# The last wo chunk's parts and the next rows' last quarter in VectorE's order, in a two-layer graph kernel

## The chip, the cores and the metric

The kernel runs on one core of a Trainium2 chip. The metric is the device time of one execution in microseconds. Before the change it is 2554.0 us, the median of three runs (2552.22 to 2556.43); the profiled execution has a span of 2553.1 us at a granted TensorE clock of 0.995.

## The reference

64 graphs of 256 nodes with 512 features, one adjacency matrix, two layers, each with a residual and a LayerNorm. Layer 0 is masked attention with 8 heads, layer 1 a plain graph convolution:

```python
q = (x @ Wq + bq).reshape(b, n, H, HD)          # k and v alike
scores = jnp.einsum('bqhd,bkhd->bhqk', q, k) / jnp.sqrt(jnp.float32(HD))
scores = scores + (1.0 - adj)[None, None, :, :] * -1000000000.0
attn = jax.nn.softmax(scores, axis=-1)
out = jnp.einsum('bhqk,bkhd->bqhd', attn, v).reshape(b, n, d)
x = layernorm(x + out @ Wo + bo)
y = jnp.einsum('nm,bmd->bnd', adj, x)
x = layernorm(x + jnp.einsum('bnd,do->bno', y, weight) + bias)
```

Everything is float32.

## The kernel before, in words

**Precision.** The five weight products (v, q, k, wo and the last weight l) are made of parts. An operand is cut into a high part, a low part (the remainder, scaled) and a correction called diff, all in the round float format that TensorE takes. A product of 512 columns is then three products that add up in one PSUM bank: low times one weight part, high times another, diff times the third. `near` (L317) issues the first two, twelve or eight matmuls in groups of four, and has ScalarE scale the bank (L326); `far` (L328) issues the third and evicts the bank. For wo and l the eviction is VectorE's: `r += bank` with a sum for the LayerNorm (L338); at the fourth chunk `norm` follows, whose first step is the mean (L436) and whose squares run on ScalarE (L444).

**Parts.** For wo and l the stationary operand is the attention's output or the convolution's, cut in four chunks. `chunk_parts` (L284) makes a chunk's parts with three VectorE operations, cut (L168), clow (L169) and cdiff (L174), and ScalarE's copy of the cut is chigh (L298). The pools hold one `cut`, three chunks of chigh and clow, and four cdiff. For v, q and k the operand is the transposed input of the pair: `x_t` transposes a quarter (L264), `x_parts` cuts it (L168, L169), `x_diff` (L174) makes its third part; ScalarE copies its high part (L278).

**Work and its order.** Two graphs make a pair, and there are 32 pairs. A window w (of 1 to 30) works on three pairs at once: wo and the convolution of pair w - 1, attention of pair w, and v, q, k of pair w + 1, with the parts of pair w + 2's input. Attention is four units (two groups of heads by two graphs). For a unit, `scores` (L359) puts eight matmuls in each of two halves (L367), ScalarE takes the exponentials (L371), and VectorE multiplies each half by the adjacency mask (L376, `masked`), then adds the halves (L382, `summed`). `values`, at the next unit's slot, sums that over the keys on TensorE (L394), multiplies with v (L402) and divides on VectorE (L412 to L418).

**Who decides the order.** In the windows 1 to 30 the order on TensorE, ScalarE and VectorE is that in which the program issues (a manual schedule). `between(w)` (L540) writes the steps of a window as one list. `block` is one near plus whatever `far` has been owed for longest (up to two stay owed); `caught_up(1)`, the step f1, pays all but one. After a block, a slot or a convolution step comes a tick; `later(n, f)` runs f at the nth tick. That places the masks: the first half's mask at the tick right after the slot, the second's one tick later (L372), the sum one tick after that. `PENDING` carries the fourth quarter of the next input's parts from one window into the next (three steps; twelve in window 1).

**Around the change.** A window begins with the slot of unit 0, then the parts of wo's third chunk (`co[2:3]`), the block of chunk 0, f1 (which pays the third product of the last l chunk of the previous pair, called l3 here), the parts of wo's last chunk (`co[3:]`), the block of chunk 1, the pending quarter, and the blocks of chunks 2 and 3. Four PSUM banks serve all these products in turn, four others serve scores and values.

Of the kernel before, what the change touches and what calls it, by code (L numbers as in the profile page):

```python
# [43 lines left out]
def fast(tc, x, adj, wq, bq, wk, bk, wv, bv, wo, bo, w1, b1, out):  # L44
# [6 lines left out]
    NP = B // 2  # L51
# [78 lines left out]
    def raw_weight(name, tiles, queue):  # L130

        for i in range(3):
            SCRATCH[name, i] = scratch.tile([P, DC, D], F32, name=f"{name}{i}")
        n = DC // len(tiles)
        for i, t in enumerate(tiles):
            for k in range(n):
                RAW[name, i * n + k] = t[:, k]
            w = SOURCE[name][i * n * P:(i + 1) * n * P]
            if name == "o":


                for a in range(n):
                    queue.dma_start(t[:, a], w.rearrange("(h a i) e -> a h i e", h=4, a=2)[a])
            else:
                queue.dma_start(t, w.rearrange("(c p) e -> p c e", p=P))
# [79 lines left out]
    def later(n, f, *args):  # L225
        due.append([n, f, args])
# [132 lines left out]
    def scores(p, u):  # L359
        g, b = UNITS[u]  # L360
        for kc in range(NC):

            sc = [ps_at.tile([P, 2, N], F32, name="at") for s in range(2)]
            for a in range(2):
                for s in range(2):
                    r = slice(s * HD, (s + 1) * HD)
                    nc.tensor.matmul(sc[s][:, a, :], K[p, g][r, a, b, kc * P:(kc + 1) * P], Q[p, g][r, a, b, :],  # L367
                                     start=True, stop=True)
            e = E[p, u, kc] = one.tile([P, 2, 2, N], F32, name=f"e{kc}")
            for s in range(2):  # L370
                nc.scalar.activation(e[:, s], sc[s], AF.Exp, scale=qscale)  # L371
            later(1 + kc, masked, p, u, kc)  # L372

    def masked(p, u, kc):
        e = E[p, u, kc].rearrange("p s a n -> p (s a) n")
# [164 lines left out]
    def between(w):  # L540

        ahead, behind = w + 1, w - 1
        b = lambda name: [(block, name, behind if name in "ol" else ahead, j) for j in range(4)]
        v, q, k, o, l = (b(n) for n in "vqkol")
        c = lambda name, p: [(chunk_parts, name, p, j) for j in range(4)]
        y = [(adj_x, behind, i) for i in range(4)]
        bo_steps = [(with_bo, w, b) for b in range(2)]
        x_steps = [(x_t, w + 2, i) for i in range(4) if w + 2 < NP]
        x1 = [[s for f in (x_t, x_parts) for s in [(f, w + 2, i)] if w + 2 < NP] for i in range(4)]
        x2 = [[(x_diff, w + 2, i)] if w + 2 < NP else [] for i in range(4)]  # L550
        slot, f1 = [None], [(caught_up, 1)]
        f0 = [(caught_up,)]
        split = lambda name: [(split_w, name, i) for i in range(4)]
        mixed = lambda m, n: [s for pair in zip(m, n) for s in pair]
        halves_tiles = lambda: [one.tile([P, 2, D], F32, name=f"hl{i}") for i in range(2)]
        if w == -1:
            return [(x_t, 0, i) for i in range(4)] + mixed(v, split("v")) + mixed(q, split("q")) + [(adj_t,)] + \
                mixed(k, x_steps)
        if w == 0:
            raw_weight("o", halves_tiles(), nc.sync)  # L560
            PENDING[:] = [s for m, n in zip(x1, x2) for s in m + n]
            return slot + mixed(v, split("k")) + slot + q[:3] + split("o") + [(bv_wo,), (load_w, 3)] + \
                [(lambda: raw_weight("l", halves_tiles(), nc.sync),)] + slot + q[3:] + k[:2] + split("l") + \
                [(load_r, 0)] + slot + k[2:] + bo_steps + c("o", w)[:2] + \
                [(load_w, 3), (load_r, 1)]
        co, cl = c("o", behind), c("l", behind)
        seq = slot + co[2:3] + o[:1] + f1 + co[3:] + o[1:2] + PENDING[:6] + o[2:] + PENDING[6:] + slot + v + q[:1] + slot + q[1:] + f1 + \
            y[:1] + f0 + y[1:2] + k[:1] + (cl[:1] if w < NP - 2 else []) + y[2:] + f0 + bo_steps + slot + k[1:2] + \
            (cl[1:2] if w < NP - 2 else [])
        PENDING[:] = x1[3] + x2[3]  # L570
        if w == NP - 2:
            co = c("o", w)
            return seq + k[2:3] + co[:1] + k[3:] + co[1:2] + [(block, "o", w, 0)] + cl[:1] + [(block, "o", w, 1)] + cl[1:2]
        seq += k[2:3] + cl[2:3] + k[3:] + x1[0] + l[:1] + f1 + x2[0] + x1[1] + x2[1] + l[1:2] + cl[3:] + \
            l[2:3] + c("o", w)[:1] + x1[2] + x2[2] + l[3:] + f1 + c("o", w)[1:2]
        return seq

    PENDING = []

    def slot(before, unit):  # L580
        if before[0] >= 0:
            values(*before)
        scores(*unit)
# [11 lines left out]
    def window(w):  # L595
        steps(between(w), [(w - 1, 3)] + [(w, u) for u in range(4)])
# [235 lines left out]
```

## Time and profile before

| | |
|---|---|
| time, median of three | 2554.0 us |
| span of the profiled execution | 2553.1 us |
| busy: TensorE, VectorE, ScalarE, GpSimd | 2496.0, 1872.6, 1705.7, 382.4 us |
| moved | 600.25 MB, mean 235 GB/s |
| TensorE's wait for clow, whole run | 24.6 us in 33 times, longest 2.2 us |
| mean of a mask (L376), of a residual (L338) | 1221, 687 ns |
| mean of a 128x512 wo or l matmul | 391 to 401 ns |

Busy time counts what an engine executed; a matmul's row is longer than the distance to the next one, since matmuls are pipelined. A row of a timeline gives start, length, engine, line and operation, output and inputs with their shapes, the number of instructions merged, and in brackets the idle time before it and what ended it. A row of the waits gives who waited for whom, the time in total, how often, and the longest.

### The profile page before, as it was taken

To read this page: it belongs to the slowest core of one execution; us is meant where nothing else is said; L and a number is where in the kernel's file an instruction comes from. 1 tells how busy PE (TensorE), PEld (TensorE's weight loads), DVE (VectorE), ACT (ScalarE), POOL (GpSimd) and SP (SyncE) were. 2 spreads that over 40 slices of the span, in tenths; PEclk is the share of its full clock that TensorE was granted. 3 is DMA by queue.
4 is the path that set the end of the run, shared out by engine and by line. 5 is a ranking of instruction groups with operands and counts; after the bars stand their busy time and mean duration, and the time that the engine had idled before them with its cause. 6 is when DMAs were issued, how large, how long until landed. Compare 5 with 4: busy or idle time off the path is not lost.

```text
span 2553.1 us, 42184 instructions
## 1 busy us (share of the span) xinstructions
PE 2496.0 (98%) x15806; PEld 1886.6 (74%) x15806; DVE 1872.6 (73%) x3239; ACT 1705.7 (67%) x3206; POOL 382.4 (15%) x793
## 2 busy tenths in 40 slices
PE   8999999999999999999999999999999999999997
PEld 4477777777777777777777777777777777777765
DVE  4676787677886677876767876768876778866786
ACT  4557666776666766666776667766667766677755
POOL 0111111111111111111111111111111111111101
PEclk9999999999999999999999999999999999999998
DMA  7868778778788687777787787787787787777711
GB/s 205 284 201 273 235 232 259 240 244 243 240 256 247 236 263 232 235 250 252 231 274 226 232 259 243 240 262 234 246 246 247 251 247 233 247 254 229 257 68 51
DMA packets 375744, 600.25 MB, mean 235 GB/s; under 512 B 273520, under 2 KB 273776, under 8 KB 317552
## 3 DMA queue, kind: packets, MB, share of 16 engines
q0 software_dynamic: 65232, 475.03, 51.9%
q1 hardware_dynamic: 309760, 121.42, 22.0%
q8 instruction: 127, 2.08, 0.3%
q10 hardware_dynamic: 544, 1.05, 0.1%
q14 instruction: 81, 0.66, 0.1%
HBM read 548.15 MB, written 49.28 MB: 234 GB/s over the span
## 4 chain that ended last, share of the span: by engine, by line
PE 70%; DVE 25%; issue 3%; DMA 1%; ACT 0%; POOL 0%; SPq 0%; DVEq 0%; ACTq 0%
PE mm L314 50%; PE at L367 7%; PE at L402 6%; PE mm L512 5%; DVE clow L169 4%; DVE r L338 3%; DVE cdiff L174 3%; DVE diff L174 2%; DVE cut L168 2%; PE at L394 2%; DVE e L376 2%; DVE low L169 2%; DVE xT L264 2%; DVE x L168 1%; DVE o L418 1%
## 5 line engine op out<-in xcount | busy, mean ns | idle before, releaser
L326 ACT ACTIVATE mm<-mm 128x512 f32<-128x512 f32 x616 | 357.8, 581 | 356.7 <-PE mm L314 356.6
L376 DVE TENSOR_TENSOR e<-e,adjT 128x1024 f32<-128x1024 f32 x256 | 307.6, 1221 | 34.2 <-ACT e L371 34.2
L314 PE MATMUL mm<-wr,clow 128*128 128x512 f32 x1024 | 285.1, 401 | 25.1 <-DVE clow L169 24.6
L371 ACT ACTIVATE e<-at 128x512 f32<-128x512 f32 x512 | 265.2, 604 | 52.9 <-PE at L367 52.9
L314 PE MATMUL mm<-wr,chigh 128*128 128x512 f32 x1024 | 279.9, 396 | 0.7
L314 PE MATMUL mm<-wr,cdiff 128*128 128x512 f32 x1024 | 269.6, 391 | 5.9 <-ACT mm L326 5.9
L314 PE MATMUL mm<-low,wr 128*128 128x512 f32 x960 | 265.1, 398 | 0.0
L314 PE MATMUL mm<-high,wr 128*128 128x512 f32 x960 | 257.2, 390 | 0.0
L367 PE MATMUL at<-qT,kT 64*128 64x256 f32 x2048 | 256.6, 389 | 0.1
L314 PEld LDWEIGHTS mm<-wr,clow 128*128 128x128 f32 x1024 | 188.7, 190 | 86.6 <-DVE clow L169 38.3
L314 PE MATMUL mm<-diff,wr 128*128 128x512 f32 x960 | 248.5, 391 | 0.0
L402 PE MATMUL at<-e,v 128*32 128x256 f32 x4096 | 246.9, 381 | 0.0
L367 PEld LDWEIGHTS at<-qT,kT 64*128 64x128 f32 x2048 | 190.6, 186 | 67.7 <-issue 53.0
L499 DVE TENSOR_TENSOR hl<-r,hl 128x512 fp32r<-128x512 f32 x122 | 84.3, 691 | 203.4 <-ACT hl L498 203.4
L314 PEld LDWEIGHTS mm<-wr,chigh 128*128 128x128 f32 x1024 | 191.5, 189 | 53.0 <-ACT chigh L298 14.2
L314 PEld LDWEIGHTS mm<-wr,cdiff 128*128 128x128 f32 x1024 | 192.5, 188 | 48.1 <-ACT mm L326 7.8
L444 ACT ACTIVATE z<-r,mean 128x512 bf16<-128x512 f32 x240 | 172.6, 719 | 76.2 <-DVE mean L436 71.2
L314 PEld LDWEIGHTS mm<-low,wr 128*128 128x128 f32 x960 | 173.6, 188 | 51.6 <-issue 19.9
L338 DVE SCALAR_TENSOR_TENSOR r<-mm,r 128x512 f32<-128x512 f32 x240 | 160.4, 687 | 69.6 <-PE mm L314 69.6
L314 PEld LDWEIGHTS mm<-high,wr 128*128 128x128 f32 x960 | 180.3, 188 | 38.4
L476 ACT ACTIVATE r<-r,less,rstd 128x512 f32<-128x512 f32 x248 | 200.4, 808 | 6.1 <-DVE less L469 6.1
L314 PEld LDWEIGHTS mm<-diff,wr 128*128 128x128 f32 x960 | 176.3, 188 | 33.6
(123 smaller groups left out, 3985.0 us busy)
## 6 DMA issues: line engine op xcount, KB each, us to landing
wr<-o POOLq DMA_DIRECT2D x93, 1024.0 KB, 6.3
wr<-v POOLq DMA_DIRECT2D x90, 1024.0 KB, 6.4
wr<-q POOLq DMA_DIRECT2D x90, 1024.0 KB, 6.5
wr<-k POOLq DMA_DIRECT2D x90, 1024.0 KB, 7.3
wr<-l POOLq DMA_DIRECT2D x90, 1024.0 KB, 7.6
x<-in_x_dram SPq DMA_DIRECT2D x496, 64.0 KB, 6.4
r<-in_x_dram SPq DMA_DIRECT2D x31, 1024.0 KB, 5.3
out_dram<-r SPq DMA_DIRECT2D x60, 512.0 KB, 6.5
```

Source lines behind the costliest of these rows:

```text
L169: nc.vector.tensor_tensor(low, a, cut, op=OP.subtract)
L174: nc.vector.scalar_tensor_tensor(diff, low.bitcast(F32), -(FINE + 1), a, op0=OP.mult, op1=OP.add)
L314: nc.tensor.matmul(pm, *operands(name, p, j, i, k), start=k == 0 and i == begins, stop=k == DC - 1, skip_group_check=True)
L326: nc.scalar.activation(pm, pm, AF.Copy, scale=1 + 1 / FINE)
L338: nc.vector.scalar_tensor_tensor(r, pm, 1.0, r, op0=OP.mult, op1=OP.add, accum_out=ST[p, name][:, j:j + 1])
L367: nc.tensor.matmul(sc[s][:, a, :], K[p, g][r, a, b, kc * P:(kc + 1) * P], Q[p, g][r, a, b, :], start=True, stop=True)
L371: nc.scalar.activation(e[:, s], sc[s], AF.Exp, scale=qscale)
L376: nc.vector.tensor_tensor(e, e, mask[:, kc:kc + 1, :].to_broadcast([P, 4, N]), op=OP.mult)
L402: nc.tensor.matmul(at[h * 32:(h + 1) * 32, a, :], V[p, b][:, kc, col:col + 32], e[kc][:, h % 2, h // 2, :], start=kc == 0, stop=kc == NC - 1)
L444: nc.scalar.activation(waste, R[p][j // 2][:, j % 2], AF.Square, bias=mean[:, j:j + 1], accum_out=squares[:, j:j + 1])
L476: nc.scalar.activation(r, r, AF.Identity, scale=rstd, bias=less)
L512: nc.tensor.matmul(pm[:, j, :], hl[:, i, mc, j * P:(j + 1) * P], adjT[:, mc, :], start=mc == 0 and i == 0, stop=mc == NC - 1 and i == 1)
```

## The change

Two edits. In windows whose pair is 2 to 30, the second mask of the first unit comes at the third tick instead of the second, so it falls behind the second block; and the parts of the last wo chunk are issued ahead of f1, so directly behind the third chunk's on VectorE. With the mask, the sum goes one tick later too. The pending quarter of the next rows' parts goes behind the block of chunk 2 instead of behind that of chunk 1; window 1, where twelve steps are pending, keeps its places. The purpose is to have the last chunk's parts ready when TensorE comes to its block.

```diff
@@ scores
-            later(1 + kc, masked, p, u, kc)
+
+            later(1 + kc * (1 + (u == 0 and 1 < p < NP - 1)), masked, p, u, kc)
@@ between
+        x_now = (PENDING[:6], [], PENDING[6:]) if w == 1 else ([], PENDING[:], [])
         co, cl = c("o", behind), c("l", behind)
-        seq = slot + co[2:3] + o[:1] + f1 + co[3:] + o[1:2] + PENDING[:6] + o[2:] + PENDING[6:] + slot + v + q[:1] + slot + q[1:] + f1 + \
+        seq = slot + co[2:3] + o[:1] + co[3:] + f1 + o[1:2] + x_now[0] + o[2:3] + x_now[1] + o[3:] + x_now[2] + slot + v + q[:1] + slot + q[1:] + f1 + \
             y[:1] + f0 + y[1:2] + k[:1] + (cl[:1] if w < NP - 2 else []) + y[2:] + f0 + bo_steps + slot + k[1:2] + \
             (cl[1:2] if w < NP - 2 else [])
```

## The prediction

> **What bounds the kernel now.** I read the page's busy times first, then who waited for whom on TensorE, then the chain of waits in order of time, then the timelines of TensorE, VectorE and ScalarE through one window. A window is one pair of graphs; its start repeats every 77.37 us (TensorE's stall of 1066.42 returns at 1143.80), and the middle 29 windows (w = 2 to 30) are alike.
>
> ```profile
> PE 2496.0 (98%) x15806; PEld 1886.6 (74%) x15806; DVE 1872.6 (73%) x3239; ACT 1705.7 (67%) x3206; POOL 382.4 (15%) x793
> ...
> PE 70%; DVE 25%; issue 3%; DMA 1%; ACT 0%; POOL 0%; SPq 0%; DVEq 0%; ACTq 0%
> ```
>
> TensorE is nearly always busy, yet a quarter of the chain lies on VectorE: somewhere in each window TensorE hands the chain to VectorE and takes it back. TensorE's waits between 500 and 2000 us, some 19.4 windows, name the place; this is the whole answer:
>
> ```profile
> PE mm L314 <- DVE clow L169: 12.1, 20, 0.6
> ```
>
> One wait per window, 0.6 us, and nothing else. The timeline of TensorE shows what is held:
>
> ```profile
> 1062.93 1.07 PE L314 MATMUL mm<-wr,clow 128*128 128x512 f32 x4
> 1063.84 1.07 PE L314 MATMUL mm<-wr,chigh 128*128 128x512 f32 x4
> 1064.74 1.07 PE L314 MATMUL mm<-wr,cdiff 128*128 128x512 f32 x4
> 1066.42 1.20 PE L314 MATMUL mm<-wr,clow 128*128 128x512 f32 x4 [0.61 <-DVE clow L169]
> 1067.65 1.19 PE L314 MATMUL mm<-wr,chigh 128*128 128x512 f32 x4
> 1068.68 1.08 PE L314 MATMUL mm<-wr,cdiff 128*128 128x512 f32 x4
> 1069.69 0.64 PE L394 MATMUL at<-sm,ones 128*32 128x256 f32 x8
> ```
>
> The first three rows are chunk 2 of wo (near, then the third product of chunk 0), the next three chunk 3 (near, then the third product of chunk 1), the last the next unit's sums of exponentials. Groups in flow start 0.91 us apart. The stall costs more than 0.61: chunk 3 should start at 1064.74 + 0.91 = 1065.65 and starts 0.77 later; its chigh group starts 1.23 after clow (ScalarE writes chigh only at 1066.98 to 1067.60), 0.32 too late; the refill adds 0.12 to cdiff. Without any wait L394 would come at 1065.65 + 0.91 + 0.91 + 1.0 = 1068.46 (the last step as in the row, 1068.68 to 1069.69). So the window loses 1.23 us. VectorE over the same stretch:
>
> ```profile
> 1062.67 0.69 DVE L174 SCALAR_TENSOR_TENSOR cdiff<-clow,o 128x512 fp32r<-128x512 f32 x1
> 1063.28 1.22 DVE L376 TENSOR_TENSOR e<-e,adjT 128x1024 f32<-128x1024 f32 x1
> 1064.42 0.68 DVE L338 SCALAR_TENSOR_TENSOR r<-mm,r 128x512 f32<-128x512 f32 x1
> 1065.03 0.08 DVE L338 DVE_READ_ACCUMULATOR r<-mm,r 128x1 f32 x1
> 1065.14 0.17 DVE L436 TENSOR_SCALAR mean<-sums 128x4 f32<-128x4 f32 x1
> 1065.22 0.42 DVE L168 TENSOR_SCALAR cut<-o 128x512 int32<-128x512 int32 x1
> 1065.67 0.69 DVE L169 TENSOR_TENSOR clow<-o,cut 128x512 fp32r<-128x512 f32 x1
> 1066.40 0.69 DVE L174 SCALAR_TENSOR_TENSOR cdiff<-clow,o 128x512 fp32r<-128x512 f32 x1
> 1067.01 1.22 DVE L382 TENSOR_TENSOR sm<-e,e 128x1024 f32<-128x1024 f32 x1
> ```
>
> VectorE has no gap here: chunk 3's low part stands behind the second mask (L376), the previous pair's last residual (L338, "r of l3" below) and the mean. Its stretch began when TensorE released a buffer to it at 1045.31 (the wait "DVE diff L174 <- PE mm L314", 28 times, 0.33 us each). So the two engines keep their distance from window to window, and what TensorE gains at L394 is gained in the period, if nothing between L394 and the next 1045.31 + 77.37 is tighter.
>
> **What the skill says.** The Trainium skill, "PSUM — Partial Sum Buffer", section "Engine vs sequencer instructions": VectorE's and ScalarE's queues are strict FIFO and matmuls start and complete in program order. The trace agrees: cdiff of chunk 1, ready since the last window, sits behind clow of chunk 3 till 1068.68. "Perfetto Trace Analysis", section "DVE / Act Engine Instruction": an instruction's end is its write acknowledged, and the semaphore's way to the others lies outside. Here clow starts at 1065.67, ends at 1066.36 and TensorE starts at 1066.42: 0.06 us more. "VectorE: DVE Perf Modes", section "The DRAIN you can't avoid", says that the next operation waits for the pipe to empty; the trace shows starts 0.61 us apart for a 128x512 operation followed by an independent one and 0.73 before its consumer, although each row says 0.69. I count starts.
>
> **The change, part by part.** It removes and adds no instruction. TensorE, GpSimd and the DMA queues keep their order. In windows 2 to 30 (u = 0 and 1 < p < 31) VectorE's order becomes: parts of chunk 2, parts of chunk 3, r of l3, mean, second mask, r of chunk 0, sum, then the next rows' last quarter (xT, x, low, diff), r of chunk 1. On ScalarE chigh of chunk 3 comes before the first two squares instead of behind them, and the copy of the next rows' high part behind the scaling of chunk 3 instead of in front of it. Window 1 keeps its order, since its mask is not delayed and its pending steps stay put.
>
> VectorE from 1063.28, with the starts measured above (cut 0.45, clow 0.73, cdiff 0.61, r 0.61, read accumulator 0.11, mean 0.08, mask 1.14): cut 1063.28, clow 1063.73, cdiff 1064.46, r of l3 1065.07, mean 1065.79, mask 1065.87, r of chunk 0 1067.01, and, behind its accumulator read, which took nothing extra between two residuals earlier in the trace, the sum at 1067.62. Do the moved ones wait? Cut needs chigh of chunk 2 read (ScalarE 1061.94 to 1062.58, past). Clow takes the buffer of chunk 0 (three of them), free by about 1060.3. Cdiff takes that of l3 (four), read by TensorE at 1060.21 to 1061.28. r of chunk 0 needs cdiff of chunk 0, done at 1065.81. None waits.
>
> Chunk 3 is then ready: clow at 1064.42; chigh on ScalarE directly behind the scaling at 1063.13, so at about 1063.7 to 1064.3. The 0.77 and the 0.32 fall away. Two other waits appear.
>
> First, chunk 3 takes the PSUM bank of l3 (four banks in turn: l3, chunks 0, 1, 2), which r of l3 frees. Before, that was done at 1065.1; now it starts at 1065.07 and releases TensorE 0.75 later (as clow did, 1065.67 to 1066.42), at 1065.82: 0.17 behind 1065.65. With one refill (1.03) L394 would come at 1065.82 + 1.03 + 0.91 + 1.0 = 1068.76.
>
> Second, L394 needs the sum. Before it had ended at 1068.23, 1.46 early; now it starts at 1067.62, 0.61 later, because r of chunk 0 was put in front of it. In the one place where the trace shows TensorE waiting for a sum, it started at 115.01 and L394 at 116.37: 1.36. So L394 comes at 1067.62 + 1.36 = 1068.98, the later of the two. Behind L394 stand the values, the scores of unit 1 and the whole rest, all in TensorE's queue. The gain is 1069.69 - 1068.98 = 0.71 us per window, times 29 = 20.6 us. Bounds: if the sum releases 0.2 sooner, the bank's 1068.76 holds (0.93, 27 us); if each of the seven moved operations costs 0.04 more, as dependent pairs do, 0.43 (12.5 us).
>
> The later block for the next rows' quarter costs nothing: its low part now starts at 1069.96 instead of 1069.35, and v reads it after the scores, at about 1073.2. ScalarE: the mean is 0.65 later, so the four squares and both scalings run from 1066.06 to 1070.22, the high part to 1070.74, zc to 1071.1; vc is wanted at 1071.4 (L402's end, 0.71 earlier than 1072.1). That margin shrinks from 1.1 to 0.3 us but stays. VectorE's lag behind TensorE is taken up by its waits of 0.27 and 1.49 us at 1074 to 1077. Weights and rows are as before: TensorE waits for no transfer in these windows.
>
> **Rivals.** *Full gain:* if VectorE's sum and r of l3 release sooner than I count, the whole 1.23 us goes: 35.7 us, 2518. For it: 0.5 us decides. Against: the queue has no gap to draw in. *The wait only changes hands:* the sum, or vc on ScalarE with its thin 0.3 us, comes later still and L394 or the scores hold most of what chunk 3 gave: 0 to 0.4 us per window, 2542 to 2554. For it: VectorE is continuously busy from 1045 to 1074, and the same work stands before L394, with one residual more. *Slower:* the moved parts wait in front of the mask. If clow of chunk 3 had to wait for chunk 2's buffer (TensorE done with it at 1064.8), all behind it comes 1.07 later, the sum releases L394 at 1070.05, 0.36 later than before: 29 x 0.36 = 10 us, 2564. Against: the buffers are counted above.
>
> **How the numbers follow.** My forecast, 0.4 to 1.0 us per window, 0.62: 2554.0 - 20.6 = 2533.4. Full gain 0.15, hands changed 0.15, slower 0.08. 0.2% is 5.1 us, 0.18 us per window; half of the third case passes it: faster 0.85, same 0.09, slower 0.06. The range 2518 to 2548 leaves out part of the full gain, the weak half of the third case and the slower one, about 0.2.
>
> **What would show it.** Right: the wait for clow gone from TensorE in windows 2 to 30; in its place about 0.2 us at L394 for the sum (L382), perhaps a trace of a wait for r (L338); a period of 76.66 us; VectorE's and TensorE's busy times unchanged. Wrong: no wait at L394 (then full gain), waits of scores on ScalarE's vc, VectorE idle before a cut or clow, or TensorE waiting for clow of chunk 2, which has only 0.25 us to spare (ready at 1062.63, read at 1062.93).

## The result and the profile after

The changed kernel takes 2539.22 us (median of four, 2537.62 to 2540.18) against 2555.22 us for the kernel before in the same comparison: ratio 0.9938, 95% interval 0.9921 to 0.9956, 16.0 us faster. The forecast was 2533.4 us, 20.6 us faster; the direction and the place were right, the gain was taken 4.6 us too large.

The page of the changed kernel, busy times and chain by engine:

```profile
PE 2492.1 (98%) x15806; PEld 1896.3 (75%) x15806; DVE 1870.2 (74%) x3239; ACT 1708.7 (67%) x3206; POOL 382.5 (15%) x793
...
PE 70%; DVE 25%; issue 3%; ACT 1%; DMA 0%; POOL 0%; DVEq 0%; SPq 0%; ACTq 0%
```

Busy times are as before, and so are the chain's shares: TensorE still hands the chain to VectorE in each window. What it waits for there has changed. TensorE's waits from 500 to 2000 us, the whole answer:

```profile
PE at L395 <- DVE sm L383: 0.5, 3, 0.2
PE mm L314 <- DVE r L338: 0.2, 1, 0.2
```

The 12.1 us for clow are gone; a sum and a residual are named instead, but only where the gap in the matmul rows is wide enough to be counted. The weight loads name the residual in every window; from the same stretch:

```profile
PEld mm L314 <- DVE r L338: 11.3, 20, 0.6
```

The regular form shows in TensorE's timeline (lines after L371 have moved by one):

```profile
1059.35 1.07 PE L314 MATMUL mm<-wr,cdiff 128*128 128x512 f32 x4
1060.56 1.20 PE L314 MATMUL mm<-wr,clow 128*128 128x512 f32 x4
1061.60 1.08 PE L314 MATMUL mm<-wr,chigh 128*128 128x512 f32 x4
1062.52 1.08 PE L314 MATMUL mm<-wr,cdiff 128*128 128x512 f32 x4
1063.72 0.64 PE L395 MATMUL at<-sm,ones 128*32 128x256 f32 x8
```

Two short stalls stand where one long one was. Chunk 3's clow group comes 1.21 us behind the group ahead, where flow is 0.91: 0.30 for the bank of l3. L395 comes 1.20 behind the last group, where flow is 1.0: 0.20 for the sum. VectorE's rows over the same stretch:

```profile
1057.27 0.69 DVE L174 SCALAR_TENSOR_TENSOR cdiff<-clow,o 128x512 fp32r<-128x512 f32 x1
1057.88 0.42 DVE L168 TENSOR_SCALAR cut<-o 128x512 int32<-128x512 int32 x1
1058.40 0.69 DVE L169 TENSOR_TENSOR clow<-o,cut 128x512 fp32r<-128x512 f32 x1
1059.20 0.69 DVE L174 SCALAR_TENSOR_TENSOR cdiff<-clow,o 128x512 fp32r<-128x512 f32 x1
1059.81 0.68 DVE L338 SCALAR_TENSOR_TENSOR r<-mm,r 128x512 f32<-128x512 f32 x1
...
1060.62 1.22 DVE L377 TENSOR_TENSOR e<-e,adjT 128x1024 f32<-128x1024 f32 x1
1061.75 0.68 DVE L338 SCALAR_TENSOR_TENSOR r<-mm,r 128x512 f32<-128x512 f32 x1
...
1062.36 1.22 DVE L383 TENSOR_TENSOR sm<-e,e 128x1024 f32<-128x1024 f32 x1
```

Cdiff of the third chunk starts at 1057.27 here and at 1062.67 in the profile before; I use this offset of 5.40 us to put both on the clock of before. The order is the forecast one and there is no gap. But clow starts 0.52 after cut, not 0.45, and cdiff 0.80 after clow, not 0.73. Everything behind is 0.14 to 0.15 late: r of l3 at 1065.21 (worked out: 1065.07), the sum at 1067.76 (1067.62), L395 at 1069.12 (1068.98).

The period, taken from one window's bias row (`r<-r,bo`) to the next, falls from 77.37 to 76.80 us: 0.57 times 29 windows is 16.5 us. The profiled spans differ by 15.8, since the first such row comes 0.9 us later in this profile (120.12 against 119.23), a start that lies between 117.9 and 121.4 in all the profiles here.

The question left is the 0.14 us. Theory A: clow and cdiff of the last chunk must each see that TensorE has done with an old buffer. Both buffers are long free, but the wait is one more entry in VectorE's queue. The chain of waits of the changed kernel, from the third chunk's cdiff on, has rows of that kind, DVEq (start, length, what; those around them are left out):

```profile
1058.34 0.02 DVEq L169
...
1058.40 0.70 DVE clow L169
...
1059.14 0.02 DVEq L174
...
1059.20 0.69 DVE cdiff L174
```

Theory B: the loss comes from the bank of l3, TensorE's 0.30, taken as 0.31 below. A second question is whether bank and sum are all that is left.

### The profile page after: what moved, and what is told of

Read it like the earlier page. It is cut to its first block, busy times and chain, and to the rows that moved or that the text cites. A ratio compares the mean times of both kernels' runs of the same rounds, so it can differ in the third digit from the quotient of the medians.

```text
span 2537.3 us, 42184 instructions
## 1 busy us (share of the span) xinstructions
PE 2492.1 (98%) x15806; PEld 1896.3 (75%) x15806; DVE 1870.2 (74%) x3239; ACT 1708.7 (67%) x3206; POOL 382.5 (15%) x793
## 4 chain that ended last, share of the span: by engine, by line
PE 70%; DVE 25%; issue 3%; ACT 1%; DMA 0%; POOL 0%; DVEq 0%; SPq 0%; ACTq 0%
PE mm L314 49%; PE at L367 7%; PE at L403 6%; PE mm L513 5%; DVE clow L169 5%; DVE cdiff L174 4%; DVE r L338 3%; DVE diff L174 2%; DVE cut L168 2%; PE at L395 2%; DVE low L169 2%; DVE xT L264 2%; DVE x L168 1%; DVE o L419 1%; DVE e L377 1%
## 5 line engine op out<-in xcount | busy, mean ns | idle before, releaser
L371 ACT ACTIVATE e<-at 128x512 f32<-128x512 f32 x512 | 265.2, 604 | 53.2 <-PE at L367 53.2
L403 PEld LDWEIGHTS at<-e,v 128*32 128x32 f32 x4096 | 139.9, 110 | 82.4 <-issue 1.5
```

The lines of the kernel that those rows point to most:

```text
L403: nc.tensor.matmul(at[h * 32:(h + 1) * 32, a, :], V[p, b][:, kc, col:col + 32], e[kc][:, h % 2, h // 2, :], start=kc == 0, stop=kc == NC - 1)
```

## The experiments

Each kernel is the changed one with one or two edits. Period is the median distance of the bias rows in its profile, before being 77.37 and the changed kernel 76.80.

| kernel | time, us | ratio to before | period expected (A), us | period measured, us |
|---|---|---|---|---|
| mask only, e2 | 2534.63 | 0.9929 (0.9912 to 0.9946) | 76.66 | 76.67 |
| quarter back, e3 | 2633.92 | 1.0314 (1.0297 to 1.0332) | 79.3 | 79.34 and 80.98, mostly in turn |
| no mask delay, e4 | 2565.97 | 1.0045 (1.0028 to 1.0062) | 77.72 | 77.73 |
| sum at once, e5 | 2529.80 | 0.9909 (0.9892 to 0.9925) | 76.59 | 76.57 |
| both gates open, e6 | 2521.83 | 0.9875 (0.9859 to 0.9891) | 76.17 | 76.23 |
| fifth cdiff, e7 | 2536.09 | 0.9930 (0.9914 to 0.9947) | 76.73 | 76.74 |

The kernel before stood at 2553.84 us beside e2 to e5 and at 2553.71 beside e6 and e7. Between neighbours the periods decide; times that differ by some 2 us do not.

### Without the two buffer waits

```diff
-... o[:1] + co[3:] + f1 + o[1:2] ...
+... o[:1] + f1 + co[3:] + o[1:2] ...
```

> The last chunk's parts go back behind f1; the delayed second mask and the moved quarter stay. VectorE's order is then: third chunk's parts, r of l3, mean, last chunk's parts, second mask, r of chunk 0, sum. The two buffer waits on TensorE in front of clow and cdiff of the last chunk are gone, since the wait of r of l3 covers them. Theory A (the 0.14 us per window that the prediction lacked are these two waits, 0.07 each, in VectorE's queue, although the buffers were long free, and the sum sets when L395 starts): clow 0.45 after cut and cdiff 0.73 after clow instead of 0.52 and 0.80; no wait for a bank any more; L395 still waits for the sum, at 1068.98 on the clock of the profile before; period 77.37 - 0.71 = 76.66 us, 20.6 us under the kernel before, 4 us under the changed one. Theory B (the 0.14 are the wait of the last chunk for the bank of l3, which costs TensorE 0.31 us in the changed kernel): with the bank free all of that comes back, period 76.80 - 0.31 = 76.49, 9 us under the changed kernel.

The period is 76.67. VectorE's rows of e2:

```profile
1055.67 0.42 DVE L168 TENSOR_SCALAR cut<-o 128x512 int32<-128x512 int32 x1
1056.13 0.69 DVE L169 TENSOR_TENSOR clow<-o,cut 128x512 fp32r<-128x512 f32 x1
1056.85 0.69 DVE L174 SCALAR_TENSOR_TENSOR cdiff<-clow,o 128x512 fp32r<-128x512 f32 x1
```

The starts are 0.46 and 0.72 apart again. TensorE's rows of the same window:

```profile
1056.34 1.07 PE L314 MATMUL mm<-wr,cdiff 128*128 128x512 f32 x4
1057.24 1.07 PE L314 MATMUL mm<-wr,clow 128*128 128x512 f32 x4
1058.15 1.15 PE L314 MATMUL mm<-wr,chigh 128*128 128x512 f32 x4
1059.13 1.07 PE L314 MATMUL mm<-wr,cdiff 128*128 128x512 f32 x4
1060.57 0.64 PE L395 MATMUL at<-sm,ones 128*32 128x256 f32 x8 [0.37 <-DVE sm L383]
```

The bank's stall is gone (0.90 to clow), yet theory B's 0.31 does not come back: L395 waits 0.37 for the sum. The gain over the changed kernel is 0.13, the two buffer waits' worth. So the swap of the last chunk's parts with f1, one part of the change, costs 0.13 us a window; the delayed mask, with the quarter moved out of the sum's way, brings all of the gain and more.

### One buffer wait alone

```diff
-bo_s, b1_s = on_all(bo, "bo"), on_all(b1, "b1")
+bo_s = b1_s = on_all(bo, "bo")
...
-differences = pool("differences", 4)
+differences = pool("differences", 5)
```

> The changed kernel with five cdiff buffers instead of four; for the room the last layer's bias shares the tile of the first's, so the second layer adds the wrong bias with the same instruction, and one small load at the start is left out. The wait on TensorE in front of cdiff of the last chunk is gone, that in front of clow stays. Theory A (each such wait costs VectorE 0.07 us in its queue though the buffer is free): cdiff 0.73 after clow instead of 0.80, clow still 0.52 after cut, period 76.73, 2 us under the changed kernel. Theory B (the longer starts belong to the order of the operations, a cut following a cdiff directly): 76.80, as the changed kernel.

VectorE's rows of e7, the order of operations that of the changed kernel:

```profile
1056.96 0.42 DVE L168 TENSOR_SCALAR cut<-o 128x512 int32<-128x512 int32 x1
1057.49 0.69 DVE L169 TENSOR_TENSOR clow<-o,cut 128x512 fp32r<-128x512 f32 x1
1058.22 0.69 DVE L174 SCALAR_TENSOR_TENSOR cdiff<-clow,o 128x512 fp32r<-128x512 f32 x1
```

Clow keeps its 0.53, cdiff is back at 0.73, and the period falls by 0.06. The order alone is therefore not the cause; the wait is. Its entry in the queue can be counted. The answers for the lines L169 and L174 list the queue's semaphore entries; for L169 in the changed kernel:

```profile
L169 DVEq EVENT_SEMAPHORE  x84: 21/21/21, 29.5 to 2502.2; - x84
```

and in e2:

```profile
L169 DVEq EVENT_SEMAPHORE  x55: 21/21/21, 30.6 to 2496.9; - x55
```

55 in the kernel before too: 29 more, one per window from 2 to 30. L174 goes from 76 to 105 and back to 76 in e2, and to 77 in e7, where L169 has 82. A further buffer for chigh and clow was not tried, so clow's share of the 0.14 rests on e2, where both entries go together.

What the entry waits for is not the buffer. The operands in the packed trace name each instruction's semaphores. In the changed kernel the entries ahead of clow and cdiff wait for the semaphore that VectorE's own operations raise, so for the operation just before; clow and cdiff themselves carry the wait for TensorE, which is long satisfied. In the kernel before and in e2 they carry VectorE's wait and have no entry. The wait for the buffer is met and holds nothing up; but beside it the other wait stands in an entry of its own, which starts 0.04 us after cut's row ends (1058.30 to 1058.34), and clow starts 0.06 after that.

The profile before already had this price, on the parts of the next rows. Two places with such an entry:

```profile
1043.76 0.43 DVE L168 TENSOR_SCALAR x<-xT 128x512 int32<-128x512 int32 x1
1044.29 0.69 DVE L169 TENSOR_TENSOR low<-xT,x 128x512 fp32r<-128x512 f32 x1
...
1047.25 0.69 DVE L169 TENSOR_TENSOR low<-xT,x 128x512 fp32r<-128x512 f32 x1
1048.04 0.69 DVE L174 SCALAR_TENSOR_TENSOR diff<-low,xT 128x512 fp32r<-128x512 f32 x1
```

Low starts 0.53 after x here and 0.46 in the 87 places of that trace without an entry; diff starts 0.79 to 0.80 after low in 58 places with one and 0.73 in 66 without.

### The quarter in front of the sum

```diff
-... if w == 1 else ([], PENDING[:], [])
+... if w >= 1 else ([], PENDING[:], [])
```

> Only the pending quarter of the next rows' parts goes back behind the block of chunk 1, in all windows. Theory A (the sum on VectorE sets L395): transpose, cut, low and diff of the quarter, 0.73 + 0.47 + 0.72 + 0.61 = 2.53 us of starts, now stand in front of the sum; L395 comes 2.5 us later than in the changed kernel, period about 79.3 us, about 57 us above the kernel before, with 2.7 us of TensorE's idle time per window at L395. Theory B (the order of the quarter is free, only chunk 3 counts): as the changed kernel, 76.80.

TensorE's row at L395 in two windows of e3, a period apart:

```profile
1103.65 0.64 PE L395 MATMUL at<-sm,ones 128*32 128x256 f32 x8 [2.68 <-DVE sm L383]
1104.08 1.94 PE L403 MATMUL at<-e,v 128*32 128x256 f32 x32
...
1182.99 0.64 PE L395 MATMUL at<-sm,ones 128*32 128x256 f32 x8 [2.69 <-DVE sm L383]
1183.42 3.05 PE L403 MATMUL at<-e,v 128*32 128x256 f32 x32
```

The wait and the shorter period (79.34) are as worked out: the sum sets L395, and the moved quarter is what makes the delayed mask possible. The time is 80 us above the kernel before and not 57, because nearly every second window (13 in all) is 1.64 us longer: after its wait TensorE runs slow (the values take 3.05 us for 1.94). That is taken up in the last section.

### The bank of l3

```diff
-later(1 + kc * (1 + (u == 0 and 1 < p < NP - 1)), masked, p, u, kc)
+later(1 + kc, masked, p, u, kc)
```

> Only the delay of the second mask is undone; the last chunk's parts stay ahead of f1. VectorE's order: third chunk's parts, second mask, last chunk's parts, r of l3, mean, sum, r of chunk 0. Theory A (the last chunk must wait for the bank that r of l3 frees): clow is ready at 1065.69 on the clock of the profile before, but the bank only at 1067.10; L395 at 1067.10 + 1.03 + 0.91 + 1.0 = 1070.04, period 77.72, some 10 us above the kernel before; TensorE's wait is named r (L338). Theory B (only the parts count): chunk 3 starts at 1065.7, L395 at 1068.6, period 76.3, 31 us under the kernel before.

TensorE's rows of e4:

```profile
992.40 1.07 PE L314 MATMUL mm<-wr,cdiff 128*128 128x512 f32 x4
994.75 1.20 PE L314 MATMUL mm<-wr,clow 128*128 128x512 f32 x4 [1.28 <-DVE r L338]
```

Period 77.73, and the time is 12.1 us above the kernel before. On the clock of before (cdiff of the third chunk at 990.33 here, so 72.34 later) the last chunk's clow starts at 1064.94 instead of 1065.67, yet TensorE starts chunk 3 at 1067.09 instead of 1066.42, because the residual that frees its bank stands behind them. Undoing the other half of the change (e2) makes it faster; undoing this half makes it slower than no change.

### The sum at once

```diff
-later(1, summed, p, u)
+(summed(p, u) if u == 0 and 1 < p < NP - 1 else later(1, summed, p, u))
```

> The changed kernel, with the first unit's sum issued directly behind its second mask in windows 2 to 30, ahead of r of chunk 0. Theory A (two gates, the bank at chunk 3 and the sum at L395, the sum the later): the sum leaves TensorE at about 1068.65 on the clock of the profile before, the bank now gates: L395 at 1065.97 + 1.03 + 0.91 + 1.0 = 1068.91 instead of 1069.12; period 76.59, 6 us under the changed kernel; no wait at L395. Theory B (the bank alone sets the time): 76.80, as the changed kernel.

TensorE's rows of e5:

```profile
1056.00 1.20 PE L314 MATMUL mm<-wr,clow 128*128 128x512 f32 x4
...
1057.94 1.07 PE L314 MATMUL mm<-wr,cdiff 128*128 128x512 f32 x4
1058.94 0.64 PE L395 MATMUL at<-sm,ones 128*32 128x256 f32 x8
```

L395 follows in flow (1.00); the bank's stall stays (clow 1.21 behind the group at 1054.79). Period 76.57: taking r of chunk 0 out of the sum's way brings 0.23 us a window, which the bank alone as a gate would not have given.

### Both gates open

The edits of e2 and e5 together.

> The delayed mask and the moved quarter of the change, the last chunk's parts behind f1 as before it, and the first unit's sum directly behind its second mask in windows 2 to 30. VectorE's order: third chunk's parts, r of l3, mean, last chunk's parts, second mask, sum, r of chunk 0. Theory A (bank and sum are the only two gates): the bank is free at 1064.0 on the clock of the profile before, chunk 3 starts in flow at 1065.65, the sum lets L395 go at 1065.87 + 1.26 + 1.36 = 1068.49, flow gives 1068.46: the whole loss of 1.2 us per window is gone, period 76.17, 35 us under the kernel before and 18 us under the changed one. Theory B (ScalarE, whose chigh of the last chunk stands behind two squares again, holds chunk 3): chigh at 1066.5 to 1067 gates the second group; L395 at 1068.9 or later, period 76.6 or more.

TensorE's rows of e6:

```profile
1052.08 1.07 PE L314 MATMUL mm<-wr,cdiff 128*128 128x512 f32 x4
1052.98 1.07 PE L314 MATMUL mm<-wr,clow 128*128 128x512 f32 x4
1053.89 1.15 PE L314 MATMUL mm<-wr,chigh 128*128 128x512 f32 x4
1054.87 1.08 PE L314 MATMUL mm<-wr,cdiff 128*128 128x512 f32 x4
1055.88 0.64 PE L395 MATMUL at<-sm,ones 128*32 128x256 f32 x8
```

Its weight load for chunk 3's chigh:

```profile
1053.84 0.75 PEld L314 LDWEIGHTS mm<-wr,chigh 128*128 128x128 f32 x4 [0.21 <-ACT chigh L298]
```

No wait of a matmul is listed for e6 between 500 and 2000 us. The groups flow; only cdiff comes 0.98 behind chigh instead of 0.91, because the weight load of chigh waits 0.21 for ScalarE, which writes it behind two squares. That is theory B's effect, at 0.07 us and not 0.4. The time is 31.9 us under the kernel before and, by the ratios, 0.6% under the changed one. This version beats both.

## Why the prediction was right, and where it fell short

**The bound.** Right: e6, which removes the wait for clow without new gates, gains 1.14 us a window of the 1.23 that the prediction read from TensorE's rows; 0.07 of the rest is chigh.

**Two new gates.** Right: bank and sum, in this order, the sum the later. The bank was worked out as a stall of 0.17 and is 0.30, since the residual comes 0.14 later for the reason given next; the sum was worked out as 0.22 after it and is 0.20. e4 and e3 show each gate alone, e6 that there is no third of weight.

**"Do the moved ones wait? ... None waits."** This is the step that failed, and the size with it. No buffer holds the moved operations up, as the prediction counted. But it gave them the distances measured ahead of the change, cut to clow 0.45 and clow to cdiff 0.73, and in the new order they are 0.52 and 0.80: each carries a wait for TensorE, and its wait for the operation before goes into an entry of its own. In the kernel before, r of l3 stood ahead of these parts and had waited for TensorE already; in e2, where it does so again, the entries and the loss are gone. 0.14 times 29 is 4.1 us: 20.6 less 4.1 is 16.5, and 16.0 was measured. The lower bound in the prediction (0.04 on each of seven operations) took the result in, but for another reason: the cost is 0.07 on two.

**The moved quarter at no cost.** Right as to its new place: no wait of v for it. In its old place beside a delayed mask it would have cost 2 us a window and more (e3).

**ScalarE's thin margin.** Right: vc starts after a gap of 0.32 us, as worked out, and the scores do not wait.

**Rivals.** The full gain did not come, because the sum and the bank released as counted; it needs r of chunk 0 behind the sum and r of l3 ahead of the parts (e6). A part of the wait did change hands: e2, with the sum as its gate, stands 0.44 us a window behind e6. The slower case did not come, for the buffers were free; e4 is slower for a reason that it did not name, parts in front of the residual that frees the bank.

## What to carry to other kernels

When work is pulled forward on a queue without gaps, write down everything that it overtakes, and ask of each who waits for it: here two operations, a residual that frees a PSUM bank and a sum that starts the next stage, each came late enough to hold TensorE; with the two queue entries they kept 0.57 us of the 1.14 that e6 gains. Look also at the waits that the new order needs on each moved instruction: a wait for another engine, though long satisfied, cost 0.07 us where it pushed the wait for the operation before into a queue entry of its own. The distance with such an entry stood in the profile before, at another line. Undoing the halves of a change one at a time can show that one half carries it and the other costs.

## What the runs showed of the hardware that was not expected

A VectorE instruction that needed both TensorE and the operation just before it had an entry of its own in the queue for the second of these. The entry's row is 21 ns, but the next start moved by 0.07 us (cut to clow 0.52 against 0.45, clow to cdiff 0.80 against 0.73). An entry that waits for another engine only had no such price: z (L413) follows cdiff by 0.61 us in the 29 places where an entry for ScalarE stands ahead of it, the distance of independent operations. The Trainium skill, "VectorE: DVE Perf Modes", section "The DRAIN you can't avoid", reports that a semaphore after each operation cost nothing extra; that measurement does not speak of a second wait, and here one cost 0.07 us.

In e3 TensorE ran slow after 13 of its 29 waits of 2.7 us. The view by stretches of time of e3, around the wait without a slow stretch and the wait with one (columns: stretch, its length, busy time and instructions of five engines, granted TensorE clock, DMA share, GB/s):

```profile
1098.76:1102.17 3.41, 2.22 (x10) 1.49 (x8) 3.31 (x6) 3.35 (x10) 1.05 (x2) 1.00 0.36 108
1102.17:1105.58 3.41, 1.93 (x36) 1.44 (x40) 2.70 (x9) 1.14 (x3) 1.03 (x1) 1.00 1.05 406
...
1180.68:1184.09 3.41, 1.10 (x21) 0.84 (x25) 2.85 (x7) 1.96 (x5) 0.47 (x1) 1.00 1.03 392
1184.09:1187.50 3.41, 3.41 (x30) 1.96 (x24) 1.46 (x4) 0.60 (x1) 0.96 (x3) 0.50 1.08 276
```

The granted clock was 0.50 from 1184.09 to 1187.50 and 1.00 in the other three. The edges are those of the trace: the 13 slow stretches each last 3.41 us and begin 160.43 us apart (once 238.94), which is 47 and 70 times 3.413. So the clock changed on a grid of 3.413 us that does not follow the windows. The same wait falls differently on it: the second leaves TensorE idle for 2.31 us of one stretch (busy 1.10 of 3.41), the first is divided by an edge into 1.19 and 1.48. Between 200 and 2450 us of e3, each of the 13 stretches with 2.09 us or more of idle time at full clock was followed by a slow one, and none with 2.00 us or less was. Two periods, 79.34 + 80.98, are close to 47 steps of the grid, which fits the alternation.

"TensorE: Matmul & The Clock Gate", section "Part 1: The HAM clock gate (the "warmup" mystery)", has the clock fall after an idle window of about 3.4 us that runs freely. The length and the free run agree with the 3.413 us here; the window did not have to be idle throughout, since some 2.1 us of it were enough. For the changed kernel it has no weight: its waits are 0.2 to 0.3 us.
